# A graph layer's start on one core: the first loads put in one queue, and block 0's edges multiplied ahead of the weights' transposes

## The chip, the core and the metric

The kernel runs on one core of a Trainium2 chip. The core has five engines with queues of their own: PE (TensorE, matrix products; its weight loads are listed as PEld), DVE (VectorE), ACT (ScalarE), POOL (GpSimd) and SP (SyncE, which here only issues DMAs). [...] The metric is device time in microseconds (us) of one execution, as a median over runs.

## The reference, cut to what matters

There are 8192 nodes with 256 features and 131072 edges, sorted by their destination.

```python
ea  = edge_attr @ w_e + b_e                      # 131072 x 64 by 64 x 256
msg = relu(x[src] + ea)                          # a row of x for each edge
agg = segment_sum(msg, dst, num_segments=8192)
t = x + agg
h_local = bn1(relu(t @ w1 + b1) @ w2 + b2 + x)
q, k, v = split(x.reshape(256, 32, 256) @ in_w.T + in_b)   # 4 heads
h_attn = bn2(softmax(q k / 8) v @ out_w.T + out_b + x)
out = h_local + h_attn
out = bn3(out + relu(out @ m_w1 + m_b1) @ m_w2 + m_b2)
return layernorm(x + out)
```

Attention runs within groups of 32 nodes. All data is float32.

## The kernel before, in words

**Edges.** They are worked on in 128 blocks (NB) of 1024 edges. For each block:

- `gather` (L133) fetches the rows of x for the block's sources into a tile `xs`, in eight indirect DMAs that GpSimd issues, each of 128 rows of 1 KiB. Blocks 0 and 1 take their row numbers from `srcd`, loaded in small pieces at the very start (L64); all others from `srci`, which is made from `srci_r`: a cast to float (`srcf`, L193), eight PE transposes (L197), four casts back (L198). From block NX = 20 on they read `xb`, a copy of x with b_e added, so that the product with b_e is left out. There are four `xs` buffers: block b + 4 is gathered into the one that block b's messages were made from.
- `load_edges` (L148) brings the block's 64 edge attributes in four DMAs of 128 KiB into `ea` (two buffers), and `edge_transpose` (L166) turns them on DVE into `eaT` (two buffers).
- `edge_products` (L451) multiplies `eaT` with `we` on PE (L459, eight matmuls for a block; the trace shows each float32 matmul as two) and, up to block 19, adds `be` by a product with `sel` (L467).
- `edge_messages` (L478) adds `xs` on DVE (L487, two instructions) and takes the relu on ACT (L491).
- `edge_hot`, `edge_sums` and `edge_place` sum the messages by destination on PE (L510, L528) and add them to the transposed node features `xT` (L538).

`next_edges(b)` (L472) turns block b's attributes and loads those of block b + 2.

**Nodes.** They are worked on in 16 chunks of 512. `attention_front` (L274) loads `xn` (L276), turns it into `xT` on PE (L283, copies on ACT L284, L285) and makes q and k (L294); `attention_back` makes v (L308), scores (L325), the softmax and the output (L360, L372); `dense` is the rest (L391). These generators are drawn on by the class `Work` between the edge blocks.

**The copy xb.** `copy_load` (L550) loads pieces of x into `xp`, `copy_store` (L555) adds `be` on DVE (L558) and stores them.

**The order.** On PE the program's order is kept as written, and up to block NV = 26 on DVE and ACT too, once the main loop has begun; before it, and on SP, a scheduler orders by its own estimates. Every DMA of SP and ACT takes the next of eight semaphores and waits until the DMA that had it before has landed; the gathers do the same with eight of their own.

**The start.** SP issues half of srcd, the attributes of blocks 0 and 1, srci_r, dsti_r, the twelve vectors `vec_r` (L187), the attributes of blocks 2 and 3, then xn of chunks 0 and 1. ACT issues the other half of srcd, then we, be, in_r and out_r (L179 to L188). PE turns srcf, the projection weights (`turned`, L203: in_r, then out_r), the vectors and dstf, then xn of chunks 0 and 1, and only then comes block 0's `edge_products`. `turned` copies with ACT (L208). The destinations go through a cast (`dstf`, L232), two reductions (L237, L238) and a subtraction of the least (`lo`, L239) on DVE.

The main loop (L665) takes two blocks at a time up to TAIL = 104; after it a planner with due times (L697 on) orders single blocks.

Of the kernel before, what the change touches and what calls it, by code (L numbers as in the profile page):

```python
# [9 lines left out]
FP = mybir.dt.float32  # L10
# [14 lines left out]
NH = 4  # L25
# [28 lines left out]
def gnn_kernel(ctx: ExitStack, tc: tile.TileContext, x, src, dst, edge_attr, w, out):  # L54
# [102 lines left out]
                )  # L157

    gather(0)
    load_edges(0)  # L160
    gather(1)
    load_edges(1)

    eaT_of = {}

    def edge_transpose(b):  # L166
        ea = ea_of.pop(b)
        eaT = eaT_of[b] = epool.tile([P, NH * EQ, QR], FP, name="eaT", tag="eaT", bufs=2)
        nc.vector.transpose(eaT, ea[:, QR:].rearrange("p (g d) -> p g d", d=ED)[:, :, :QR])  # L169

    with tc.tile_pool(name="setup", bufs=1) as sp:


        srci_r = npool.tile([P, BE], I32, name="srci_r", tag="y")
        dsti_r = npool.tile([P, BE], I32, name="dsti_r", tag="h1")
        nc.sync.dma_start(srci_r, src.rearrange("(s e) -> s e", s=NB))
        nc.sync.dma_start(dsti_r, dst.rearrange("(s e) -> s e", s=NB))
        for h in range(2):
            nc.scalar.dma_start(we[h * ED : (h + 1) * ED, :], w["w_e"])  # L179
        nc.scalar.dma_start(be, w["b_e"][None, :].to_broadcast([P, C]))  # L180
        in_r = npool.tile([P, 3 * KC, C], FP, name="in_r", tag="m1")
        out_r = npool.tile([P, KC, C], FP, name="out_r", tag="vn")
        nc.scalar.dma_start(in_r, w["in_w"].rearrange("(o p) c -> p o c", p=P))
        vec_r = npool.tile([nrows, P], FP, name="vec_r", tag="pr")
        for v in VECS:
            r, n = col[v]
            nc.sync.dma_start(vec_r[r : r + n, :], w[v].rearrange("(r p) -> r p", p=P))  # L187
        nc.scalar.dma_start(out_r, w["out_w"].rearrange("(o p) c -> p o c", p=P))  # L188
        for b in range(2):
            edge_transpose(b)  # L190
            load_edges(b + 2)
        srcf = npool.tile([P, NH * TJ, EQ, QR], FP, name="srcf", tag="zT")
        nc.vector.tensor_copy(srcf, srci_r.rearrange("s (t r m) -> s t m r", r=QR, m=EQ))  # L193
        for h in range(NH):
            ps = bank()[:, : TJ * NB].rearrange("p (j s) -> p j s", j=TJ)
            for j in range(TJ):
                nc.tensor.transpose(ps[:, j, :], srcf[:, h * TJ + j].rearrange("s m r -> s (m r)"), ident)  # L197
            nc.vector.tensor_copy(srci[:, :, h * TJ : (h + 1) * TJ].rearrange("p s j -> p j s"), ps)  # L198


        nc.vector.memset(bd, 0.0)
# [70 lines left out]


    def attention_front(n0, st, pool, bank):  # L274
        xn = st["xn"] = pool.tile([P, TN, C], FP, name="xn", tag="xn", bufs=4)
        nc.sync.dma_start(xn, x[ds(n0, CH), :].rearrange("(t p) c -> p t c", p=P))  # L276
        yield REST
        xT = st["xT"] = pool.tile([P, KC, CH], FP, name="xT", tag="xT", bufs=4)
        hA = st["hA"] = pool.tile([P, KC, CH], FP, name="hA", tag="hA", bufs=4)
        for k in range(KC):  # L280
            ps = bank()
            for t in range(TN):
                nc.tensor.transpose(ps[:, t * P : (t + 1) * P], xn[:, t, k * P : (k + 1) * P], ident)  # L283
            nc.scalar.copy(xT[:, k, :], ps)  # L284
            nc.scalar.activation(  # L285
                hA[:, k, :], xT[:, k, :], AF.Identity, scale=s12[:, k : k + 1], bias=cA[:, k : k + 1]
            )
        yield 0.9

        qk = st["qk"] = pool.tile([P, 2 * KC, CH], FP, name="qk", tag="qk")  # L290
        for o in range(2 * KC):
            ps = bank()
            for k in range(KC):
                nc.tensor.matmul(  # L294
                    ps, inT[:, k, o * P : (o + 1) * P], xT[:, k, :], start=(k == 0), stop=(k == KC - 1)
                )
            nc.scalar.activation(qk[:, o, :], ps, AF.Identity, bias=v_("in_b", o))  # L297
            st["front"] = o == 2 * KC - 1
            yield 1.7
# [145 lines left out]
        yield 0.0  # L445


    chunk = [{} for _ in range(NCH)]
    pe_of, msg_of, oh_of, newest = {}, {}, {}, {}

    def edge_products(b):  # L451

        eaT = eaT_of.pop(b).rearrange("p (h m) r -> p h (m r)", h=NH)
        for h in range(0, NH, 2):
            pe = bank2().rearrange("p i (u c) -> p i u c", u=2)
            for u in range(2):
                for i in range(2):
                    rows = slice(i * ED, (i + 1) * ED)
                    nc.tensor.matmul(  # L459
                        pe[:, i, u, :], eaT[rows, h + u], we[rows, :],  # L460
                        start=(b >= NX or u == 0), stop=(b >= NX), skip_group_check=True,
                    )
            if b < NX:
                for u in range(2):
                    for i in range(2):
                        rows = slice(i * ED, (i + 1) * ED)
                        nc.tensor.matmul(  # L467
                            pe[:, i, u, :], sel[rows, :], be[rows, :], start=False, stop=True, skip_group_check=True
                        )
            pe_of[b, h] = pe  # L470

    def next_edges(b):  # L472
        if b < NB:
            edge_transpose(b)
        if b + 2 < NB:
            load_edges(b + 2)

    def edge_messages(b):  # L478

        xs = xs_of.pop(b)  # L480
        msg = msg_of[b] = epool.tile([P, NH, TJ, C], FP, name="msg", tag="msg", bufs=3)
        n = 2 if b < NB - 1 else 1
        for h in range(0, NH, 2):
            pe = pe_of.pop((b, h))
            for u in range(0, 2, n):
                hs = slice(h + u, h + u + n)
                nc.vector.tensor_add(  # L487
                    msg[:, hs].rearrange("p u i c -> p i u c"), pe[:, :, u : u + n, :],
                    xs[:, hs].rearrange("p u i c -> p i u c"),
                )  # L490
                nc.scalar.activation(msg[:, hs], msg[:, hs], AF.Relu)  # L491

    def edge_hot(b):

        oh = oh_of[b] = epool.tile([P, TB, WN], FP, name="oh", tag="oh", bufs=2)
        nc.vector.tensor_tensor(  # L496
            oh,
            iota_n[:, None, :WN].to_broadcast([P, TB, WN]),
            rel[:, b, :, None].to_broadcast([P, TB, WN]),
            ALU.is_equal,  # L500
        )

    def edge_sums(blocks):

        pw = pps.tile([P, 2, C], FP, name="pw", tag="pw", bufs=1)
        for i, b in enumerate(blocks):
            msg, oh = msg_of.pop(b), oh_of.pop(b)
            for j in range(TJ):
                for h in range(NH):
                    nc.tensor.matmul(  # L510
                        pw[h * WN : (h + 1) * WN, i, :], oh[:, h * TJ + j, :], msg[:, h, j, :],
                        start=(j == 0), stop=(j == TJ - 1), skip_group_check=True,
                    )
        n = len(blocks)
        ws = epool.tile([P, 2, C], FP, name="ws", tag="ws", bufs=2)
        newest["ws"] = nc.scalar.copy(ws[:, :n], pw[:, :n]).ins  # L516
        oh2 = epool.tile([P, 2, WB], FP, name="oh2", tag="oh2")
        for i, b in enumerate(blocks):
            nc.vector.tensor_scalar(oh2[:, i, :], iota_n, wrow[:, b : b + 1], None, ALU.is_equal)
        return blocks, ws, oh2  # L520

    def edge_place(blocks, ws, oh2):

        l2 = pps.tile([P, KC, C], FP, name="l2", tag="pw", bufs=1)
        last = len(blocks) - 1
        for i in range(last + 1):
            for k in range(KC):
                nc.tensor.matmul(  # L528
                    l2[:, k, i * NPB : i * NPB + WB], ws[:, i, k * P : (k + 1) * P], oh2[:, i, :],
                    start=(i == 0 and k == 0), stop=(i == last), skip_group_check=True,  # L530
                )
        n = blocks[0] * NPB - WL
        end = n + last * NPB + WB
        for c in range(max(n, 0) // CH, (min(end, N) - 1) // CH + 1):
            assert chunk[c]["v"]
            a, z = max(n, c * CH), min(end, (c + 1) * CH)
            xT = chunk[c]["xT"][:, :, a - c * CH : z - c * CH]
            newest["xT"] = nc.vector.tensor_add(xT, l2[:, :, a - n : z - n], xT).ins  # L538

    xp_of = {}  # L540


# [83 lines left out]
    with tc.manual_schedule(engines={PE}):  # L626
# [9 lines left out]
        for c in range(NCH):  # L636
            st, before, same = chunk[c], chunk[c - 1], chunk[c - 4]
            front = attention_front(c * CH, st, npool, bank)
            if c < 2:
                next(front)  # L640
                next(front)
            work.add(
                FRONT,
                lambda c=c, b=before, s=same: (c < 1 or b.get("scores"))
# [20 lines left out]
        while b < TAIL:  # L665
# [7 lines left out]
                    wt, name = ((w1, "w1"), (w2, "w2"), (mw1, "m_w1"), (mw2, "m_w2"))[i - 4]  # L673
                    nc.sync.dma_start(wt, w[name].rearrange("(k p) m -> p k m", p=P))

            edge_products(b)
            next_edges(b + 2)
            edge_messages(b)
            if waiting:
                sums = edge_sums(waiting)  # L680
            waiting = list(blocks)
# [185 lines left out]
```

## Time and profile before

| | |
|---|---|
| median of 3 runs | 1331.11 us (1328.47 to 1333.7) |
| the profiled execution | 1331.09 us |
| its span, first to last instruction | 1329.3 us |
| PE busy | 1195.2 us, 90% of the span |
| DVE busy | 784.9 us, 59% |
| ACT busy | 587.7 us, 44% |
| GpSimd (POOL) busy | 983.9 us, 74% |
| first 40 us: PE, DVE, POOL busy | 10.01, 16.43, 28.08 us |
| first 40 us: what the DMA engines moved | 224 GB/s |
| granted clock of PE, mean | 0.967 of full speed |

A row of the timeline gives the start, the duration, the engine (with a q for its queue of DMA issues), the source line, the operation, what is written from what, how many instructions were put together, and, in brackets, how long the engine was idle before and what ended that. A row of a group of instructions gives busy time and mean duration, then the idle time before them. What ended an idle time is inferred from semaphores, and where several were waited for it can name the wrong one.

### The profile page before, as it was taken

The page shows a single profiled execution, that of the slowest core. Times are in us where ns is not written, and L with a number is a line of the kernel's source. Part 1 is how long each engine was busy: PE and PEld are TensorE (multiplying, and loading weights), DVE is VectorE, ACT ScalarE, POOL GpSimd, SP SyncE. Part 2 cuts the span into 40 slices and gives each one's busy share as a digit, 9 for nine tenths or more (in the row PEclk, how much of TensorE's full clock was granted, in tenths as well). Part 3 has the DMA queues.
Part 4 walks back from the last instruction along what each step waited for, and adds up shares of the span by engine and source line. Part 5 has one row for each costly group of instructions (what it writes and reads, how often), then busy time and mean ns, then how long its engine had stood idle before and what let it go on. Part 6 is the DMA issues. An engine that isn't in the chain of part 4 may idle for free.

```text
span 1329.3 us, 21099 instructions
## 1 busy us (share of the span) xinstructions
PE 1195.2 (90%) x7795; PEld 741.0 (56%) x7795; DVE 784.9 (59%) x1339; ACT 587.7 (44%) x840; POOL 983.9 (74%) x1032
## 2 busy tenths in 40 slices
PE   2898989999998989899898988989898999999987
PEld 1566656556555556555555555545555555545655
DVE  4377555765756565755647465465646557575654
ACT  1343433454536454443435444354454444443433
POOL 6677777777777777777777777777777777777771
PEclk9899999999999989999999999989899999999998
DMA  7999966676667666666756666566566466656741
GB/s 204 320 267 299 260 199 169 169 199 167 181 160 196 157 181 167 171 177 165 190 150 185 160 176 171 157 181 167 170 169 199 138 169 186 166 163 159 192 129 47
DMA packets 148904, 240.34 MB, mean 181 GB/s; under 512 B 27934, under 2 KB 112188, under 8 KB 148028
## 3 DMA queue, kind: packets, MB, share of 16 engines
q0 software_dynamic: 49152, 134.28, 37.6%
q1 hardware_dynamic: 97196, 103.34, 28.9%
q10 hardware_dynamic: 2448, 1.32, 0.4%
q8 instruction: 63, 1.03, 0.3%
q14 instruction: 45, 0.37, 0.1%
HBM read 222.06 MB, written 16.78 MB: 180 GB/s over the span
## 4 chain that ended last, share of the span: by engine, by line
PE 38%; POOL 28%; issue 14%; DVE 9%; DMA 8%; ACT 2%; DVEq 0%; ACTq 0%; SPq 0%; POOLq 0%
POOL xs L138 28%; PE at L391 11%; PE pe L459 8%; DMA xs<-xb,srci 5%; PE at L294 5%; PE pw L510 4%; DVE msg L487 3%; PE l L528 3%; PE at L372 2%; PE pe L467 2%; PE at L308 1%; DMA xp<-in_x_dram 1%; PE at L360 1%; PE pe L325 1%; DMA in_r<-in_L_gnn_in_w_dram 1%
## 5 line engine op out<-in xcount | busy, mean ns | idle before, releaser
L138 POOL DMA_INDIRECT xs<-xb,srci x864 | 823.7, 953 | 263.2 <-issue 250.1
L491 ACT ACTIVATE msg<-msg 128x1024 f32<-128x1024 f32 (+1 forms) x258 | 270.0, 1049 | 435.5 <-DVE msg L487 432.6
L487 DVE TENSOR_TENSOR msg<-pe,xs 128x1024 f32<-128x1024 f32 (+1 forms) x258 | 305.7, 1199 | 155.4 <-DMA xs<-xb,srci 88.6
L459 PE MATMUL pe<-we,eaT 64*128 64x256 f32 x2048 | 271.0, 398 | 29.8 <-DVE msg L487 26.4
L459 PEld LDWEIGHTS pe<-we,eaT 64*128 64x128 f32 x2048 | 192.1, 191 | 118.5 <-issue 74.6
L138 POOL DMA_INDIRECT xs<-in_x_dram,srci x144 | 143.0, 993 | 48.8 <-issue 39.6
L169 DVE STREAM_TRANSPOSE eaT<-ea 128x512 f32<-128x512 f32 x128 | 90.1, 704 | 99.6 <-PE pe L459 70.9
L510 PE MATMUL pw<-msg,oh 128*32 128x256 f32 x2048 | 130.4, 389 | 6.6 <-DVE oh L496 5.0
L391 PE MATMUL at<-hA,mw 128*128 128x512 f32 (+2 forms) x304 | 123.9, 538 | 2.9 <-DVE hA L401 2.2
L294 PE MATMUL at<-xT,inT 128*128 128x512 f32 x256 | 120.9, 598 | 0.4 <-ACT xT L284 0.4
L391 PE MATMUL at<-m,mw 128*128 128x512 f32 (+2 forms) x304 | 117.5, 529 | 2.5 <-ACT qk L297 2.2
L510 PEld LDWEIGHTS pw<-msg,oh 128*32 128x32 f32 x2048 | 60.4, 111 | 69.1 <-issue 30.7
L528 PEld LDWEIGHTS l<-oh,ws 128*128 128x128 f32 x512 | 78.0, 196 | 28.4 <-issue 21.9
L528 PE MATMUL l<-oh,ws 128*128 128x160 f32 x512 | 87.9, 312 | 2.0 <-ACT ws L516 2.0
L391 PEld LDWEIGHTS at<-hA,mw 128*128 128x128 f32 x304 | 54.7, 196 | 50.5 <-issue 42.6
L391 PEld LDWEIGHTS at<-m,mw 128*128 128x128 f32 x304 | 54.2, 190 | 49.9 <-issue 44.5
L538 DVE TENSOR_TENSOR xT<-l,xT 128x96 f32<-128x96 f32 (+4 forms) x107 | 46.1, 452 | 54.2 <-PE l L528 53.9
L294 PEld LDWEIGHTS at<-xT,inT 128*128 128x128 f32 x256 | 47.0, 190 | 55.3 <-issue 51.0
L391 PE MATMUL at<-xT,w 128*128 128x512 f32 (+2 forms) x152 | 70.9, 606 | 6.9 <-DVE xT L538 6.9
L407 ACT ACTIVATE m<-at,vec 128x512 f32<-128x512 f32 (+2 forms) x76 | 46.8, 616 | 57.2 <-PE at L391 56.7
L297 ACT ACTIVATE qk<-at,vec 128x512 f32<-128x512 f32 x64 | 43.6, 684 | 62.6 <-PE at L294 62.4
L391 PE MATMUL at<-h,w 128*128 128x512 f32 (+2 forms) x152 | 64.2, 544 | 6.1 <-ACT h L398 6.1
(107 smaller groups left out, 1199.9 us busy)
## 6 DMA issues: line engine op xcount, KB each, us to landing
ea<-in_edge_attr_dram SPq DMA_DIRECT2D x512, 128.0 KB
xs<-xb,srci POOLq DMA_INDIRECT x864
xn<-in_x_dram SPq DMA_DIRECT2D x16, 512.0 KB
out_dram<-y SPq DMA_DIRECT2D x14, 512.0 KB
xp<-in_x_dram SPq DMA_DIRECT2D x10, 512.0 KB
xb<-xp SPq DMA_DIRECT2D x10, 512.0 KB
xp<-in_x_dram SPq DMA_DIRECT2D x3, 1024.0 KB
xb<-xp SPq DMA_DIRECT2D x3, 1024.0 KB
```

What stands on the lines that cost most here:

```text
L138: nc.gpsimd.indirect_dma_start(out=xs[:, h, j, :], out_offset=None, in_=x if b < NX else xb[:, :], in_offset=bass.IndirectOffsetOnAxis(ap= ...
L169: nc.vector.transpose(eaT, ea[:, QR:].rearrange("p (g d) -> p g d", d=ED)[:, :, :QR])
L294: nc.tensor.matmul(ps, inT[:, k, o * P : (o + 1) * P], xT[:, k, :], start=(k == 0), stop=(k == KC - 1))
L297: nc.scalar.activation(qk[:, o, :], ps, AF.Identity, bias=v_("in_b", o))
L391: nc.tensor.matmul(ps, wt[:, k, o * P : (o + 1) * P], act[:, k, :], start=(k == 0), stop=(k == nk - 1))
L407: nc.scalar.activation(m1[:, o, :], layer(mw1, KC, o, hA), AF.Relu, bias=v_("m_b1", o))
L459: nc.tensor.matmul(pe[:, i, u, :], eaT[rows, h + u], we[rows, :], start=(b >= NX or u == 0), stop=(b >= NX), skip_group_check=True,)
L487: nc.vector.tensor_add(msg[:, hs].rearrange("p u i c -> p i u c"), pe[:, :, u : u + n, :], xs[:, hs].rearrange("p u i c -> p i u c"),)
L491: nc.scalar.activation(msg[:, hs], msg[:, hs], AF.Relu)
L510: nc.tensor.matmul(pw[h * WN : (h + 1) * WN, i, :], oh[:, h * TJ + j, :], msg[:, h, j, :], start=(j == 0), stop=(j == TJ - 1), skip_group_ ...
L528: nc.tensor.matmul(l2[:, k, i * NPB : i * NPB + WB], ws[:, i, k * P : (k + 1) * P], oh2[:, i, :], start=(i == 0 and k == 0), stop=(i == la ...
L538: newest["xT"] = nc.vector.tensor_add(xT, l2[:, :, a - n : z - n], xT).ins
```

## The change: what it does

The loads of the start all go through SP, in the order srci_r, block 0's attributes, we, block 1's attributes, be, dsti_r, the vectors, in_r, xn of chunk 0, out_r, xn of chunk 1. Loading xn becomes a function of its own, called here for chunks 0 and 1. The attributes of blocks 0 and 1 are turned after srci is made, and block 0's products, the turn of block 2's attributes (with the load of block 4's) and block 0's messages are written ahead of the turning of the weights. The main loop leaves these three calls out for block 0. `edge_products` to `edge_place` stand earlier in the file, unchanged.

```diff
     gather(0)
-    load_edges(0)
     gather(1)
-    load_edges(1)
...
+    def load_nodes(n0, st, pool):
+        xn = st["xn"] = pool.tile([P, TN, C], FP, name="xn", tag="xn", bufs=4)
+        nc.sync.dma_start(xn, x[ds(n0, CH), :].rearrange("(t p) c -> p t c", p=P))
+
     with tc.tile_pool(name="setup", bufs=1) as sp:
         srci_r = npool.tile([P, BE], I32, name="srci_r", tag="y")
+        nc.sync.dma_start(srci_r, src.rearrange("(s e) -> s e", s=NB))
+        load_edges(0)
         dsti_r = npool.tile([P, BE], I32, name="dsti_r", tag="h1")
-        nc.sync.dma_start(srci_r, src.rearrange("(s e) -> s e", s=NB))
+        for h in range(2):
+            nc.sync.dma_start(we[h * ED : (h + 1) * ED, :], w["w_e"])
+        load_edges(1)
+        nc.sync.dma_start(be, w["b_e"][None, :].to_broadcast([P, C]))
         nc.sync.dma_start(dsti_r, dst.rearrange("(s e) -> s e", s=NB))
-        for h in range(2):
-            nc.scalar.dma_start(we[h * ED : (h + 1) * ED, :], w["w_e"])
-        nc.scalar.dma_start(be, w["b_e"][None, :].to_broadcast([P, C]))
         in_r = npool.tile([P, 3 * KC, C], FP, name="in_r", tag="m1")
         out_r = npool.tile([P, KC, C], FP, name="out_r", tag="vn")
-        nc.scalar.dma_start(in_r, w["in_w"].rearrange("(o p) c -> p o c", p=P))
...
             nc.sync.dma_start(vec_r[r : r + n, :], w[v].rearrange("(r p) -> r p", p=P))
-        nc.scalar.dma_start(out_r, w["out_w"].rearrange("(o p) c -> p o c", p=P))
-        for b in range(2):
-            edge_transpose(b)
-            load_edges(b + 2)
+        nc.sync.dma_start(in_r, w["in_w"].rearrange("(o p) c -> p o c", p=P))
+        load_nodes(0, chunk[0], npool)
+        nc.sync.dma_start(out_r, w["out_w"].rearrange("(o p) c -> p o c", p=P))
+        load_nodes(CH, chunk[1], npool)
...
+        for b in range(2):
+            edge_transpose(b)
+            load_edges(b + 2)
+        edge_products(0)
+        next_edges(2)
+        edge_messages(0)
...
     def attention_front(n0, st, pool, bank):
-        xn = st["xn"] = pool.tile([P, TN, C], FP, name="xn", tag="xn", bufs=4)
-        nc.sync.dma_start(xn, x[ds(n0, CH), :].rearrange("(t p) c -> p t c", p=P))
-        yield REST
+        if "xn" not in st:
+            load_nodes(n0, st, pool)
+            yield REST
+        xn = st["xn"]
...
             if c < 2:
                 next(front)
-                next(front)
...
-            edge_products(b)
-            next_edges(b + 2)
-            edge_messages(b)
+            if b:
+                edge_products(b)
+                next_edges(b + 2)
+                edge_messages(b)
```

In the built program SP's order is then: srcd, srci_r, attributes of block 0, we, attributes of block 1, be, dsti_r, the vectors, in_r, xn, out_r, xn, the attributes of blocks 2 to 5, and then the first two pieces of xp, which stood right behind xn before. DVE makes srci first, then turns the attributes of blocks 0 and 1, casts and reduces the destinations, makes block 0's messages, and goes on with the destinations. From block 1's messages on, the order on PE, DVE and ACT is as before.

More of the change, by code (lines that the diff above doesn't have):

```diff
@@ L169, in edge_transpose, with edge_products @@
         nc.vector.transpose(eaT, ea[:, QR:].rearrange("p (g d) -> p g d", d=ED)[:, :, :QR])
+    pe_of, msg_of, oh_of, newest = {}, {}, {}, {}
+    def edge_products(b):
+        eaT = eaT_of.pop(b).rearrange("p (h m) r -> p h (m r)", h=NH)
+        for h in range(0, NH, 2):
+            pe = bank2().rearrange("p i (u c) -> p i u c", u=2)
+            for u in range(2):
+                for i in range(2):
+                    rows = slice(i * ED, (i + 1) * ED)
+                    nc.tensor.matmul(
+                        pe[:, i, u, :], eaT[rows, h + u], we[rows, :],
+                        start=(b >= NX or u == 0), stop=(b >= NX), skip_group_check=True,
+                    )
+            if b < NX:
+                for u in range(2):
+                    for i in range(2):
+                        rows = slice(i * ED, (i + 1) * ED)
+                        nc.tensor.matmul(
+                            pe[:, i, u, :], sel[rows, :], be[rows, :], start=False, stop=True, skip_group_check=True
+                        )
+            pe_of[b, h] = pe
@@ new lines, in next_edges, with edge_messages @@
+    def next_edges(b):
+        if b < NB:
+            edge_transpose(b)
+        if b + 2 < NB:
+            load_edges(b + 2)
+    def edge_messages(b):
+        xs = xs_of.pop(b)
+        msg = msg_of[b] = epool.tile([P, NH, TJ, C], FP, name="msg", tag="msg", bufs=3)
+        n = 2 if b < NB - 1 else 1
+        for h in range(0, NH, 2):
+            pe = pe_of.pop((b, h))
+            for u in range(0, 2, n):
+                hs = slice(h + u, h + u + n)
+                nc.vector.tensor_add(
+                    msg[:, hs].rearrange("p u i c -> p i u c"), pe[:, :, u : u + n, :],
+                    xs[:, hs].rearrange("p u i c -> p i u c"),
+                )
+                nc.scalar.activation(msg[:, hs], msg[:, hs], AF.Relu)
@@ new lines, in edge_hot, with edge_sums @@
+    def edge_hot(b):
+        oh = oh_of[b] = epool.tile([P, TB, WN], FP, name="oh", tag="oh", bufs=2)
+        nc.vector.tensor_tensor(
+            oh,
+            iota_n[:, None, :WN].to_broadcast([P, TB, WN]),
+            rel[:, b, :, None].to_broadcast([P, TB, WN]),
+            ALU.is_equal,
+        )
+    def edge_sums(blocks):
+        pw = pps.tile([P, 2, C], FP, name="pw", tag="pw", bufs=1)
+        for i, b in enumerate(blocks):
+            msg, oh = msg_of.pop(b), oh_of.pop(b)
+            for j in range(TJ):
+                for h in range(NH):
+                    nc.tensor.matmul(
+                        pw[h * WN : (h + 1) * WN, i, :], oh[:, h * TJ + j, :], msg[:, h, j, :],
+                        start=(j == 0), stop=(j == TJ - 1), skip_group_check=True,
+                    )
+        n = len(blocks)
+        ws = epool.tile([P, 2, C], FP, name="ws", tag="ws", bufs=2)
+        newest["ws"] = nc.scalar.copy(ws[:, :n], pw[:, :n]).ins
+        oh2 = epool.tile([P, 2, WB], FP, name="oh2", tag="oh2")
+        for i, b in enumerate(blocks):
+            nc.vector.tensor_scalar(oh2[:, i, :], iota_n, wrow[:, b : b + 1], None, ALU.is_equal)
+        return blocks, ws, oh2
@@ new lines, in edge_place @@
+    def edge_place(blocks, ws, oh2):
+        l2 = pps.tile([P, KC, C], FP, name="l2", tag="pw", bufs=1)
+        last = len(blocks) - 1
+        for i in range(last + 1):
+            for k in range(KC):
+                nc.tensor.matmul(
+                    l2[:, k, i * NPB : i * NPB + WB], ws[:, i, k * P : (k + 1) * P], oh2[:, i, :],
+                    start=(i == 0 and k == 0), stop=(i == last), skip_group_check=True,
+                )
+        n = blocks[0] * NPB - WL
+        end = n + last * NPB + WB
+        for c in range(max(n, 0) // CH, (min(end, N) - 1) // CH + 1):
+            assert chunk[c]["v"]
+            a, z = max(n, c * CH), min(end, (c + 1) * CH)
+            xT = chunk[c]["xT"][:, :, a - c * CH : z - c * CH]
+            newest["xT"] = nc.vector.tensor_add(xT, l2[:, :, a - n : z - n], xT).ins
@@ L171, in gnn_kernel @@
+    chunk = [{} for _ in range(NCH)]
+    def load_nodes(n0, st, pool):
+        xn = st["xn"] = pool.tile([P, TN, C], FP, name="xn", tag="xn", bufs=4)
+        nc.sync.dma_start(xn, x[ds(n0, CH), :].rearrange("(t p) c -> p t c", p=P))
     with tc.tile_pool(name="setup", bufs=1) as sp:
         srci_r = npool.tile([P, BE], I32, name="srci_r", tag="y")
+        nc.sync.dma_start(srci_r, src.rearrange("(s e) -> s e", s=NB))
+        load_edges(0)
         dsti_r = npool.tile([P, BE], I32, name="dsti_r", tag="h1")
-        nc.sync.dma_start(srci_r, src.rearrange("(s e) -> s e", s=NB))
+        for h in range(2):
+            nc.sync.dma_start(we[h * ED : (h + 1) * ED, :], w["w_e"])
+        load_edges(1)
+        nc.sync.dma_start(be, w["b_e"][None, :].to_broadcast([P, C]))
@@ L198, in gnn_kernel @@
             nc.vector.tensor_copy(srci[:, :, h * TJ : (h + 1) * TJ].rearrange("p s j -> p j s"), ps)
+        for b in range(2):
+            edge_transpose(b)
+            load_edges(b + 2)
+        edge_products(0)
+        next_edges(2)
+        edge_messages(0)
         nc.vector.memset(bd, 0.0)
@@ L445, in dense @@
         yield 0.0
[L448 to L538, printed above, removed]
```

## The prediction

> **What bounds the kernel.** I read the page first, then GpSimd's timeline, its waits, and the timeline of the first 60 us.
>
> ```profile
> span 1329.3 us, 21099 instructions
> ...
> PE 1195.2 (90%) x7795; PEld 741.0 (56%) x7795; DVE 784.9 (59%) x1339; ACT 587.7 (44%) x840; POOL 983.9 (74%) x1032
> ...
> L138 POOL DMA_INDIRECT xs<-xb,srci x864 | 823.7, 953 | 263.2 <-issue 250.1
> ```
>
> By busy share the tensor engine leads (90%), GpSimd has 74%. But a gather is 0.95 us of busy time and 0.30 us of "issue" that belongs to it (250.1 of 263.2 us idle): a pace of 1.25 us, and there are 1024. The gathers' own timeline tells whether that pace is ever broken (columns: start, duration, engine, what, and the idle time before):
>
> ```profile
> 4.25 1.10 POOL L138 DMA_INDIRECT xs<-in_x_dram,srcd  x1 [2.65 <-issue]
> ...
> 23.16 1.80 POOL L138 DMA_INDIRECT xs<-in_x_dram,srcd  x1 [0.30 <-issue]
> 25.87 1.47 POOL L138 DMA_INDIRECT xs<-in_x_dram,srci  x1 [0.92 <-DVE srci L198]
> 27.65 0.95 POOL L138 DMA_INDIRECT xs<-in_x_dram,srci  x1 [0.30 <-issue]
> ...
> 45.14 0.94 POOL L138 DMA_INDIRECT xs<-in_x_dram,srci  x1 [0.30 <-issue]
> 49.30 0.94 POOL L138 DMA_INDIRECT xs<-in_x_dram,srci  x1 [3.22 <-DVE msg L487]
> ...
> 73.19 2.29 POOL L138 DMA_INDIRECT xs<-in_x_dram,srci  x1 [0.30 <-issue]
> ```
>
> ```profile
> 194.43 0.94 POOL L138 DMA_INDIRECT xs<-in_x_dram,srci  x1 [0.30 <-issue]
> ...
> 197.06 0.96 POOL L138 DMA_INDIRECT xs<-in_x_dram,srci  x1 [1.68 <-DVE oh L519]
> ```
>
> The last gather starts at 1302.79. From 4.25, 1023 steps of 1.25 us come to 1283.0; 19.8 us are lost on the way. The steps shown give 1.46 us (to 25.87), 0.53 (to 27.65), 2.91 (to 49.30) and 1.38 (to 197.06), together 6.3. The rest is some forty gathers longer than 0.95 us, such as that at 73.19. After 197.06 no wait over 0.31 us is listed. From the last gather to the end are 26.5 us. So **GpSimd's queue of gathers sets the end**: what it loses, the kernel loses, as long as the buffers (xs, four of them) come free in time. That the chain of waits gives PE 38% says that PE is close behind, not that it is the bound.
>
> Why does it wait? At 25.87 for indices (srci). At 49.30 and 197.06 for an xs buffer: block 4 needs the one that block 0's two adds (L487) read, block 18 that of block 14.
>
> ```profile
> 15.26 0.43 SPq L176 DMA_DIRECT2D srci_r<-in_src_dram  x1
> ...
> 26.95 3.65 SPq L154 DMA_DIRECT2D ea<-in_edge_attr_dram  x8
> ...
> 30.64 0.98 SPq L276 DMA_DIRECT2D xn<-in_x_dram  x2
> ...
> 37.80 1.94 PE L283 MATMUL at<-ident,xn 128*128 128x128 f32 x8 [2.75 <-DMA xn<-in_x_dram]
> ...
> 46.08 0.71 DVE L169 STREAM_TRANSPOSE eaT<-ea 128x512 f32<-128x512 f32 x1 [10.11 <-DMA xp<-in_x_dram]
> 46.72 2.32 DVE L487 TENSOR_TENSOR msg<-pe,xs 128x1024 f32<-128x1024 f32 x2
> ...
> 51.70 7.13 PE L294 MATMUL at<-xT,inT 128*128 128x512 f32 x16
> ```
>
> Block 0's gathers were issued by 14.1, yet its adds ran at 46.72: PE's products of block 0 (42.26) stand behind the transposes of xn (37.80), and xn was asked for at 30.64, because SP spent 12.54 us on eight ea issues and then stood in the small vec loads until 26.95. In the later stretch the adds trail too: block 14's end at 196.8 although its gathers were issued by 164.1. Between 40 and 200 us the list of PE's waits names only 0.7 us for a DMA, so there **PE's order of work, started late, holds the buffers**.
>
> **The change part by part**, against the profiled execution (1331.09 us, of which the span is 1329.3; the median of the runs is 1331.11, so the same sum serves both).
>
> 1. srci_r becomes SP's first load after srcd: issued at about 2.7 instead of 15.26. In before it was cast at 23.06, 7.8 us after its issue; the same 7.8 make it about 10.5, the four srci copies end near 14, and gather 16 is not due until some 25. The wait of 0.92 falls to the usual 0.30: **0.6 us gained**. What is late next is nothing near: 11 us of room.
>
> 2. The casts stay beside gathers. [...] The row agrees for the casts: the gather beside the cast srcf (23.06, 1.07 us) took 1.80 instead of 0.95, the one beside dstf (25.45) 1.47. So srcf costs its 0.85 again elsewhere; dstf, half of which now fell into the wait, goes from 0.53 to 0.85: **0.3 lost**. [...]
>
> 3. Block 0's 8+8 products, its two adds and relus move ahead of the weights' transposes. They need ea0, we, be and block 0's gathers. The gathers decide: issued by 14.1, and landed within 10 us, since each gather waits for the eighth before it and no such wait shows. So the adds run at 20 to 25, and gather 32, due near 45, finds its buffer 20 us free: **2.9 us gained**. Behind these adds DVE holds the dst subtraction and the vec copy, behind the relus ACT holds the copies of in_w's transposes; both have room until the weights land.
>
> 4. Five loads go from ACT's queue to SP's. ACT saves 2.7 us of issue (0.45 to 0.60 each) before 5.65, where it next works at 27.82: worth nothing. SP pays them, but the 29 issues from srci_r to xn1, at 0.45 us or less each, are 13 us, under the transfers. Both kernels need the same 5.4 MiB (srci_r, dsti_r, ea0 to ea3, we, be, in_r, out_r, xn0, xn1) at the start; before had them all with xn1 at 40.39 (PE's second xn transposes), an average of about 150 GB/s from 2.7 us. At that rate xn1, now with 1 MiB less ahead of it, lands at about 33, and ea3, now last, at about 40.
>
> 5. So PE's order starts earlier. After: xn1's transposes end near 35.5, block 1's products (3.8 us) near 39.5, and the first L294 starts there instead of 51.70: **a lead of up to 12 us**. Block 1's adds now stand behind the eaT transposes of blocks 2 and 3, so behind ea3: 40 + 0.7 + 2.3 gives about 43.5; gather 40 needs them at 55.9. Nothing that PE consumes is missing for this lead: block 9's adds ran at 129.66, its last gather was issued at 109.9 and landed before 120.
>
> 6. The third stall: gather 144 (block 18) now arrives 3.2 us earlier, at 192.2, and needs block 14's adds done 4.6 us earlier than before; block 16's first (174.7) needs block 12's 2.9 us earlier. With a lead of 12, shrinking to perhaps 6 under way, both hold: **1.4 us gained**. From there on the order on PE, DVE and ACT is the same instruction for instruction, and in many blocks past 570 us, and in the last four, the adds end within 3 to 6 us of the block's last gather, so PE has caught up by then: all of it moves with the gathers, the last 26.5 us too.
>
> 7. SP's order further on: ea4 and ea5 now stand ahead of the xp loads, which go from 32.26 to about 42, after the transposes of block 3. With 1 MiB of ea ahead of the first pair's 1.5 they land between 55 (at 195 GB/s: the 300 GB/s of the stretch from 40 to 80 us less 105 for the gathers, 128 KiB per 1.25 us) and 60 (at 150). Their add ran at 72.39 and would now like to run at 60: it may cost DVE a microsecond of the lead, of which 7 are spare. xn2 and xn3 move from 55.69 to about 80 to 95, used at 129.77; w1 moves to about 65, used at 203.00. All hidden; without that cover each microsecond would eat the lead before it costs time.
>
> Sum: -0.6 + 0.3 - 2.9 - 1.4 = **-4.6 us**, 1331.1 - 4.6 = **1326.5**. The ends: -6 (dstf beside no gather, the adds on xp beside fewer) and 0 (no lead at all).
>
> **The rivals.** (a) The stall only moves: if PE's lead at block 12 is below 4.6 us, gathers 128 and 144 wait for xs as before, and the gain is the lead itself; at 2.5 us the time is 1328.6. For it: PE is 34 to 38 us busy of every 40 from 40 to 200, so a lead lost is not made up. Against it: the 12 us of step 5. (b) Fewer long gathers: between 70 and 185 seven gathers beside other work of DVE (73.19 and its like) cost 5.9 us over 0.95. With DVE's adds on xp at other phases half of that may go: 1326.5 - 3 = 1323.5. But the same adds still run beside gathers without a pause, so it can as well go the other way. (c) **Slower: the xp loads come late.** In DVE's fixed order the add on xp stands ahead of block 4's messages. From that add's start to the end of block 4's adds are 14.1 us in before (72.39 to 86.5), and gather 64, which waits for them, started at 90.8. A landing at 78 ends them at 92: 1.3 us late against before, which the third stall (1.4) just pays back, so this is where it decides; a landing at 86 ends them at 100, 9.4 late, and the time is 1331 + 8 = 1339. For it: they are pushed behind two more blocks of edges in a single queue, with the DMA engines' share at 1.07 and 1.02 in the stretches 40 to 80 and 80 to 120. Against it: that is 18 us over the later of the two estimates. (d) The change does not do what it says: excluded by the built order, which has block 0's products before in_r's transposes.
>
> **The numbers.** About 0.5% (6.7 us) can be told from no change here. Forecast 0.64, (a) 0.16, (b) 0.13, (c) 0.07. The range takes in (b) with 1 us of scatter below, 1322.5, and most of (a) above, to 1330.8, just short of no gain; the runs of before alone lie 5.3 us apart. Faster by over 0.5% (below 1324.4): (b) and a little of the forecast's edge, 0.19; slower (c) mostly, 0.06; the rest, 0.75, is within.
>
> **What would show it.** Gathers' timeline: no idle over 0.31 us near 25, 46 and 195, the last gather near 1298.2, and still 26.5 us behind it. DVE's first two adds at 20 to 25; PE's first L294 near 39.5; srcf cast near 10. A wait for DVE msg at gathers 40 to 150 would be (a), and a DVE idle before L558's new line, with a DMA of xp as its end, would be (c). I am wrong if the last gather starts within a microsecond of 1302.8, or if the tail behind it changes.

## The result, and the profile after

The changed kernel takes 1327.49 us (median of 22 runs, 1324.36 to 1329.69), the kernel before in the same measurement 1330.32 us (22 runs): a ratio of 0.9972, 95% interval 0.9963 to 0.998. That is 2.8 us less, where 4.6 were forecast. The profiled run took 1327.67 us.

The page of the changed kernel, its span and the row of the gathers:

```profile
span 1325.9 us, 21105 instructions
...
L138 POOL DMA_INDIRECT xs<-xb,srci x864 | 824.1, 954 | 263.2 <-issue 246.5
```

Its idle time, 263.2 us, is what it was before, to the tenth: the row holds only the 864 gathers from xb (blocks 20 to 127), and what has moved lies ahead of them and shows only in the timeline. The new line numbers: L208 is the message add, L167 the transposition eaT, L180 and L188 the products, L401 the old L294, L432 the old L325, L345 the subtraction of lo.

GpSimd's timeline of the changed kernel, at the places that the prediction named (start, duration, idle before):

```profile
8.12 1.43 POOL L138 DMA_INDIRECT xs<-in_x_dram,srcd  x1 [0.30 <-issue]
...
17.37 1.67 POOL L138 DMA_INDIRECT xs<-in_x_dram,srcd  x1 [0.30 <-issue]
...
23.09 1.71 POOL L138 DMA_INDIRECT xs<-in_x_dram,srcd  x1 [0.30 <-issue]
...
26.36 0.95 POOL L138 DMA_INDIRECT xs<-in_x_dram,srci  x1 [0.30 <-issue]
...
46.36 0.94 POOL L138 DMA_INDIRECT xs<-in_x_dram,srci  x1 [0.30 <-issue]
```

```profile
190.74 0.95 POOL L138 DMA_INDIRECT xs<-in_x_dram,srci  x1 [0.30 <-issue]
194.64 0.97 POOL L138 DMA_INDIRECT xs<-in_x_dram,srci  x1 [2.96 <-DVE oh L240]
```

The stall at gather 32 is gone (46.36, idle 0.30) and so is the wait for srci at gather 16 (26.36). But three gathers of the start are long, and gather 144 waits 2.96 us where before it waited 1.68. Everything that the gathers lose over 1.25 us a step, by place:

| place | before | after | change | forecast |
|---|---|---|---|---|
| gathers 1 to 31 | 2.14 | 2.14 | 0.0 | -0.3 |
| gather 32 | 2.91 | 0.00 | -2.91 | -2.9 |
| gathers 33 to 143 | 6.38 | 5.63 | -0.75 | 0 |
| gather 144 | 1.38 | 2.65 | +1.27 | -1.4 |
| gathers 145 to 1023 | 6.98 | 7.35 | +0.37 | 0 |
| behind the last gather | 26.5 | 25.2 | -1.35 | 0 |

(The table is the sum of each gather's start less the one before and less 1.25. With 0.03 at the first gather it comes to -3.4, the difference of the two spans.) The largest miss: gather 144 was to gain 1.4 us and lost 1.3.

Why? The head start was there. The timeline of all engines:

```profile
7.66 1.07 DVE L291 CAST srcf<-srci_r 128x1024 f32<-128x1024 int32 x1 [4.12 <-DMA srci_r<-in_src_dram]
...
20.51 2.34 DVE L208 TENSOR_TENSOR msg<-pe,xs 128x1024 f32<-128x1024 f32 x2
...
36.40 5.42 PE L401 MATMUL at<-xT,inT 128*128 128x512 f32 x12
```

PE's first L401 runs 15.3 us earlier than L294 did (51.70), and message block 6 still 13.5 us earlier (89.5 against 103.0). Block 7 is 9.4 us earlier (99.2 against 108.5), block 10 only 2.9 (145.4, 148.3), block 14, whose buffer gather 144 needs, 2.4. Its two adds, before and after:

```profile
194.47 2.32 DVE L487 TENSOR_TENSOR msg<-pe,xs 128x1024 f32<-128x1024 f32 x2
```

```profile
192.06 2.32 DVE L208 TENSOR_TENSOR msg<-pe,xs 128x1024 f32<-128x1024 f32 x2
```

Gather 144 would have come 5.1 us earlier than its buffer came free before, so it waits 2.65 of them. The lead is lost between 93 and 145 us. VectorE, then TensorE, in that stretch:

```profile
98.53 0.71 DVE L167 STREAM_TRANSPOSE eaT<-ea 128x512 f32<-128x512 f32 x1 [6.07 <-DMA ea<-in_edge_attr_dram]
...
117.44 0.71 DVE L167 STREAM_TRANSPOSE eaT<-ea 128x512 f32<-128x512 f32 x1 [2.63 <-DMA ea<-in_edge_attr_dram]
```

```profile
95.16 1.99 PE L415 MATMUL at<-inT,xT 128*128 128x256 f32 x8
100.50 3.79 PE L432 MATMUL pe<-qk 64*128 64x128 f32 x32 [3.35 <-DVE msg L208]
...
114.62 3.64 PE L231 MATMUL pw<-msg,oh 128*32 128x256 f32 x32 [4.25 <-DVE oh L217]
```

VectorE stood idle 6.07 us before the transposition at 98.53, for the edge attributes of block 9, and another 2.63 before that at 117.44, for those of block 10; before, the list of VectorE's waits had no DMA of ea between 40 and 240 us. TensorE, behind it, paused 3.35 us, and then L432 took 3.79 us where L325 had taken 2.06. The windows of 2 us say why (columns: PE, PEld, DVE, ACT, POOL busy, the granted clock, DMA share, GB/s):

```profile
98.00:100.00 2.00, 0.00 (x0) 0.00 (x0) 1.47 (x2) 0.00 (x0) 1.59 (x2) 0.96 0.92 327
100.00:102.00 2.00, 1.50 (x14) 1.53 (x16) 2.00 (x3) 1.54 (x2) 1.50 (x2) 0.50 0.73 228
102.00:104.00 2.00, 2.00 (x22) 1.99 (x20) 2.00 (x2) 1.92 (x5) 1.70 (x2) 0.50 1.09 325
104.00:106.00 2.00, 2.00 (x11) 1.78 (x8) 1.41 (x2) 1.55 (x5) 1.70 (x2) 0.50 0.80 284
106.00:108.00 2.00, 2.00 (x15) 1.56 (x16) 1.22 (x2) 0.00 (x0) 1.39 (x3) 0.83 1.07 312
```

TensorE comes out of the pause at half its clock (0.50) and stays there until about 106.7. The clock fell within the pause of 3.35 us: if it went from 1.00 to 0.50 in one step, the 0.96 of the first window puts that about 0.2 us before 100, some 2.7 us after the pause began.

And why did the edges come late? SP's queue in the changed kernel:

```profile
64.00 1.73 SPq L688 DMA_DIRECT2D w<-in_L_gnn_w_dram  x2
...
72.92 2.54 SPq L154 DMA_DIRECT2D ea<-in_edge_attr_dram  x4
75.65 1.58 SPq L688 DMA_DIRECT2D mw<-in_L_gnn_m_w_dram  x2
81.06 5.37 SPq L154 DMA_DIRECT2D ea<-in_edge_attr_dram  x4
```

The four matrices of the dense layers (w, mw: 1.5 MiB, first used at 200.5 us) are issued around the edges of block 8 (72.92), and ahead of those of block 9 (81.06 to 86.4). Before, they went out at 35 to 55 us. The diff does not touch them: the scheduler moved them. The DMA engines' mean share is 0.95 to 1.07 in each 40 us from 40 to 160 us, in both kernels.

Of the seven occasions on which the experiments ran, five had the kernel before itself at 1995 to 2034 us instead of 1329, for a reason that was not found, and the times of those ten runs (e1 to e6, e8 to e11) decide nothing here.

So two causes stood in line: **A**, the loads of the weights make the edges late and these eat the lead; **B**, the clock falls for reasons of its own. A third, **C**, is a form of A: every byte in the full stretch costs its time, wherever it stands in the queue.

### The profile page after: what moved, and what is told of

It is laid out like the page before. It is cut to its first block, busy times and chain, and to the rows that moved or that the text cites. A ratio compares the mean times of both kernels' runs of the same rounds, so it can differ in the third digit from the quotient of the medians.

```text
span 1325.9 us, 21105 instructions
## 1 busy us (share of the span) xinstructions
PE 1201.6 (91%) x7795; PEld 744.8 (56%) x7795; DVE 785.4 (59%) x1339; ACT 587.3 (44%) x840; POOL 984.2 (74%) x1032
## 3 DMA queue, kind: packets, MB, share of 16 engines
q8 instruction: 63, 1.03, 0.3%
## 4 chain that ended last, share of the span: by engine, by line
PE 39%; POOL 23%; issue 12%; DMA 12%; DVE 9%; ACT 3%; SPq 1%; DVEq 0%; POOLq 0%; ACTq 0%
POOL xs L138 23%; PE at L498 12%; PE pe L180 8%; DMA xs<-xb,srci 5%; PE at L401 5%; PE pw L231 4%; DVE msg L208 4%; PE l L249 3%; PE at L479 2%; DMA ea<-in_edge_attr_dram 2%; DMA xs<-in_x_dram,srci 2%; PE at L415 1%; PE at L467 1%; PE pe L188 1%; DMA xb<-xp 1%
## 5 line engine op out<-in xcount | busy, mean ns | idle before, releaser
L138 POOL DMA_INDIRECT xs<-xb,srci x864 | 824.1, 954 | 263.2 <-issue 246.5
L208 DVE TENSOR_TENSOR msg<-pe,xs 128x1024 f32<-128x1024 f32 (+1 forms) x258 | 305.4, 1199 | 152.3 <-DMA xs<-xb,srci 86.3
L180 PE MATMUL pe<-we,eaT 64*128 64x256 f32 x2048 | 273.5, 401 | 30.6 <-DVE msg L208 26.0
L180 PEld LDWEIGHTS pe<-we,eaT 64*128 64x128 f32 x2048 | 193.9, 192 | 120.2 <-issue 74.9
L167 DVE STREAM_TRANSPOSE eaT<-ea 128x512 f32<-128x512 f32 x128 | 90.2, 704 | 88.1 <-PE pe L180 68.0
L231 PE MATMUL pw<-msg,oh 128*32 128x256 f32 x2048 | 130.2, 388 | 5.8 <-DVE oh L217 4.3
L401 PE MATMUL at<-xT,inT 128*128 128x512 f32 x256 | 122.8, 605 | 2.0 <-ACT qk L404 1.5
L231 PEld LDWEIGHTS pw<-msg,oh 128*32 128x32 f32 x2048 | 60.0, 111 | 68.4 <-issue 29.8
L401 PEld LDWEIGHTS at<-xT,inT 128*128 128x128 f32 x256 | 47.3, 191 | 57.7 <-issue 51.2
L432 PE MATMUL pe<-qk 64*128 64x128 f32 x512 | 42.9, 321 | 31.5 <-DVE msg L208 31.5
```

What stands on the lines that cost most here:

```text
L138: nc.gpsimd.indirect_dma_start(out=xs[:, h, j, :], out_offset=None, in_=x if b < NX else xb[:, :], in_offset=bass.IndirectOffsetOnAxis(ap= ...
L180: nc.tensor.matmul(pe[:, i, u, :], eaT[rows, h + u], we[rows, :], start=(b >= NX or u == 0), stop=(b >= NX), skip_group_check=True,)
L208: nc.vector.tensor_add(msg[:, hs].rearrange("p u i c -> p i u c"), pe[:, :, u : u + n, :], xs[:, hs].rearrange("p u i c -> p i u c"),)
L231: nc.tensor.matmul(pw[h * WN : (h + 1) * WN, i, :], oh[:, h * TJ + j, :], msg[:, h, j, :], start=(j == 0), stop=(j == TJ - 1), skip_group_ ...
L401: nc.tensor.matmul(ps, inT[:, k, o * P : (o + 1) * P], xT[:, k, :], start=(k == 0), stop=(k == KC - 1))
```

## The experiments

The times of e7 and e12 count. From the other ten runs only rows are used: the lengths of single gathers, which are the same there (0.95 us), and in e9 the order. The changed kernel was not run beside e7 or e12; each is compared with before.

### The weights' loads late

```diff
-                if 4 <= i < 8:
+                if 14 <= i < 18:
...
-                    nc.sync.dma_start(wt, ...)
+                    with tc.issue_after(last_ea[b + 3]):
+                        nc.sync.dma_start(wt, ...)
```

(The loads of xn are tied to the edges of block 9 in the same way, so that they keep their place.) e2 and e5 are the same kernel, with times that decide nothing (0.9982, interval 0.9944 to 1.002; 0.9987, 0.9947 to 1.0026).

> The changed kernel with the four weights' loads put behind the edge loads of blocks 17 and 19 in SP's queue (issued at about 170 and 190 us, first use at 200.5), everything else in the same order. Theory A: as with the weights left out up to 165 us, stall at gather 144 gone, 1324.8 us (0.995); a first dense layer that waits for w1 shows on TensorE at 200 and costs the gathers nothing. Theory B: 1327.5 (0.997), clock row as in the changed kernel.

> The same kernel as e5 (the four weights' loads behind the edge loads of blocks 17 and 19 in SP's queue, at about 170 and 190 us), on another occasion, since the kernel before took some 2000 us both times. Theory A (the loads, ahead of ea 8 and ea 9 in the full DMA stage, eat the lead of the messages over the gathers): VectorE's wait of 6.07 us for ea before the transpose at 98.53 goes, message block 14 starts at 184 to 186 instead of 192.1, the stall of 2.66 us at gather 144 goes, 1324.8 us, 0.9952 of before. Theory B (TensorE's granted clock, 0.67 to 0.83 from 100 to 140 us, falls for reasons of its own and eats the lead): the ea wait goes, clock row and stall stay, 0.9972.

Measured, e7: 1323.99 us against 1328.91, a ratio of 0.9962, interval 0.9951 to 0.9973. GpSimd, and SP, in e7:

```profile
191.74 0.95 POOL L138 DMA_INDIRECT xs<-in_x_dram,srci  x1 [0.30 <-issue]
193.00 0.95 POOL L138 DMA_INDIRECT xs<-in_x_dram,srci  x1 [0.30 <-issue]
```

```profile
70.31 9.59 SPq L154 DMA_DIRECT2D ea<-in_edge_attr_dram  x8
...
170.79 2.11 SPq L690 DMA_DIRECT2D w<-in_L_gnn_w_dram  x2
...
191.04 1.29 SPq L690 DMA_DIRECT2D mw<-in_L_gnn_m_w_dram  x2
```

Gather 144 (193.00) does not wait. The edges of blocks 8 and 9 leave at 70.31 to 79.9, VectorE's waits for ea are gone from its list, TensorE does not pause at 97, message block 7 runs at 94.0 (99.2), block 8 at 108.7 (118.1), block 14 at 181.7 (192.1). That is what A expected, even 2 us better; and B falls as a cause of its own, since the half clock at 100 went with the pause. TensorE still pauses there once, 5.00 us, for oh before L231 at 108.01, as before did at 122.56, and is at half clock (0.50) until about 113.6. Of the expected 2.7 us on the changed kernel, medians show 2.1 (4.9 against 2.8 below before); the two intervals overlap, so that part rests on the trace, one execution of each. Its span is 4.2 us shorter. The gathers up to 144 explain 1.7 of them: 2.65 at gather 144 and 0.6 at the start are gained, 1.56 lost at gathers 33 to 143. Another 2.4 come from many small steps behind gather 144 (4.96 us lost there, in e12 5.16, in the changed kernel 7.35), which A did not foresee; why is open.

### The weights not loaded, or loaded first

In e1 ScalarE fills the four tiles from inT, so the dense layers compute with other numbers; in e3 the loads come with blocks 0 to 3 (both with the same tie of xn):

```diff
-                if 4 <= i < 8:
+                if 0 <= i < 4:
```

> The changed kernel without the four loads of w1, w2, mw1, mw2 (1.5 MiB at 64 to 77 us): ScalarE fills the four tiles with parts of inT instead, so the dense layers work on other numbers. All else stands in the same order on every engine and queue. Theory A (in the full DMA stage these loads, standing in SP's queue ahead of ea 8 and ea 9, make the edge blocks late, and the lead of the messages over the gathers is eaten): 1.5 MiB at the some 190 GB/s that the gathers leave of 300 are 8 us, so ea 9 is issued by 78 instead of 86, VectorE's wait for ea before the transpose at 98.53 (6.07 us) goes, message block 14 starts at 184 to 186 instead of 192.1, the stall of 2.66 us at gather 144 goes, and the time is 1324.8 us, 0.995 of before. Theory B (the granted clock of TensorE, 0.67 to 0.83 from 100 to 140 us, falls for reasons of its own): the ea waits go but the clock row stays, message block 14 still starts after 190, and the time is 1327.5, 0.997.

> The changed kernel with the four weights' loads four blocks earlier in SP's queue (about 38 to 46 us, around the first xp loads), the same bytes before 160 us. Theory A in its narrow form (the place in the queue counts: ahead of ea 8 and ea 9 it hurts, earlier the lead of 13 us covers it): lead kept, stall at gather 144 gone, 1324.8 us. Theory C (the DMA engines are full from 40 to 160 us, and every byte in that stretch costs its time wherever it stands): the xp loads and with them ea 8 and ea 9 are as late as now, message block 14 after 190, stall at gather 144 of 2 to 3 us, 1327.5; slower than the changed kernel by up to 2 us if ea 4 or ea 5 also come late enough for a second stall.

Measured: 1.0008 (0.9981 to 1.0035) and 0.9992 (0.9953 to 1.003): no verdict. What e3 was to tell, e12 told in part, with the same bytes early but a smaller lead at the start.

### The loads alone

Block 0's products and messages go back into the main loop; the single queue stays.

```diff
-        edge_products(0)
-        next_edges(2)
-        edge_messages(0)
...
-            if b:
-                edge_products(b)
-                next_edges(b + 2)
-                edge_messages(b)
+            edge_products(b)
+            next_edges(b + 2)
+            edge_messages(b)
```

Three runs of it (e8, e10, e11) have no verdict: 0.9993 (0.9962 to 1.0023), 0.9968 (0.9929 to 1.0006), 1.001 (0.9976 to 1.0044).

> The kernel of e10 once more: all first loads in SP's queue in order of need, block 0's products and messages back in the main loop, behind the weights' transposes. If the loads carry the gain: messages 0 run by about 40 (before 46.7), the stall of 2.91 us at gather 32 is gone, and the time is 0.9975 to 0.9985 of before. If the early messages carry it: messages 0 end after 45, gather 32 still waits 1 us or more, 0.999 or above. Stall at gather 144, with the weights' loads around the first xp loads (ahead of ea 6, the same bytes before 160 us): below 1.4 us if the place in the queue alone eats the lead, 2 us or more if every byte in the full DMA stage costs its time.

Measured, e12: 1324.42 us against 1329.34, 0.9967, interval 0.9955 to 0.9979: a little more than the 0.9975 to 0.9985 that was expected. VectorE's and GpSimd's timelines in e12:

```profile
36.02 2.32 DVE L208 TENSOR_TENSOR msg<-pe,xs 128x1024 f32<-128x1024 f32 x2
```

```profile
45.19 0.94 POOL L138 DMA_INDIRECT xs<-in_x_dram,srci  x1 [0.30 <-issue]
```

```profile
191.89 0.95 POOL L138 DMA_INDIRECT xs<-in_x_dram,srci  x1 [0.30 <-issue]
```

Messages 0 run at 36.02, 10.7 us earlier than before, and gather 32 (45.19) finds its buffer free: **the loads alone are enough for the whole gain**. With them, putting block 0's messages forward to 20.5 gains nothing more, since no one waits for them before 45. What the early messages would gain without the loads is not shown. And gather 144 (191.89) does not wait, though the lead at the start was smaller (first L398, the old L294, at 41.01 instead of 36.40). SP's queue, VectorE and TensorE:

```profile
48.08 2.35 SPq L685 DMA_DIRECT2D w<-in_L_gnn_w_dram  x2
50.79 0.37 SPq L685 DMA_DIRECT2D mw<-in_L_gnn_m_w_dram  x1
...
58.75 0.39 SPq L685 DMA_DIRECT2D mw<-in_L_gnn_m_w_dram  x1
...
80.57 10.54 SPq L154 DMA_DIRECT2D ea<-in_edge_attr_dram  x8
```

```profile
93.86 0.71 DVE L167 STREAM_TRANSPOSE eaT<-ea 128x512 f32<-128x512 f32 x1 [4.29 <-DMA ea<-in_edge_attr_dram]
```

```profile
95.83 1.13 PE L180 MATMUL pe<-we,eaT 64*128 64x256 f32 x8 [1.47 <-DVE msg L208]
...
101.41 2.06 PE L429 MATMUL pe<-qk 64*128 64x128 f32 x32
...
113.39 3.64 PE L231 MATMUL pw<-msg,oh 128*32 128x256 f32 x32 [4.98 <-DVE oh L217]
```

Here the scheduler issued the weights at 48 to 59, the same bytes ahead of the edges of block 8 (80.57), and these are late too: VectorE idles 4.29 us at 93.86, and message block 7 runs at 99.4, just when it does in the changed kernel (99.2). So far this fits C: with these bytes ahead, block 7 runs at some 99 in both kernels, though their leads at the start differ by 4.6 us; e7, without them, has it at 94.0. But what follows differs. TensorE pauses 1.47 us (95.83), stays at full clock (1.00), does the old L325 at 101.41 in 2.06 us, and has one long pause, the 4.98 us for oh that every kernel has here. From block 7 to block 14 it takes 87.6 us, e7 87.7, before 85.9, the changed kernel 92.9. Of the 5.3 us between the changed kernel and e12 here, 4.2 fall between blocks 7 and 8 (18.9 us against 14.8): 2.6 are VectorE's wait for the edges of block 10 (117.44), which come in time in e12, and the rest lies beside the half clock of 99.8 to 106.7. Another 1.7 fall between blocks 9 and 10, beside a further such stretch (130.6 to 134.0). So B has up to 3 us in it, though at 100 the clock fell in the pause that the late edges made. As a forecast of the time C fell: 2 us or more of stall expected, none found.

### The subtraction on ScalarE

```diff
-        nc.vector.tensor_sub(dst3, dst3, lo[...].to_broadcast(...))
+        nlo = sp.tile([P, NH], FP, name="nlo")
+        nc.vector.tensor_scalar(nlo, lo, -1.0, None, ALU.mult)
+        for h in range(NH):
+            nc.scalar.activation(dst3[:, h], dst3[:, h], AF.Identity, bias=nlo[:, h : h + 1])
```

> The changed kernel with the subtraction of lo from dst (one VectorE instruction with two SBUF inputs, 1.21 us at 22.77) done by ScalarE in four pieces with a bias. If the two SBUF inputs hold the gather beside it (1.71 us at 23.09): that gather falls to 0.95 us, the gap total of the first 30 us falls from 1.97 to 1.2 us, and, the gathers being the bound, the time falls by 0.8 us to 1326.7 (0.9966), less what the later stall at gather 144 takes back, since its slot does not come free any earlier: nothing then, 1327.5. If it was chance, the gather stays near 1.7 us.

> The changed kernel with the subtraction of lo from dst (one VectorE instruction with two SBUF inputs, 1.21 us at 22.77) done by ScalarE in four pieces with a bias, run again for the same reason. If the two SBUF inputs hold the gather beside it (1.71 us at 23.09): that gather falls to 0.95 us and the gap total of the first 30 us from 1.97 to 1.2 us; the time falls by 0.8 us to 0.9966 of before if nothing later takes it back, and stays at 0.9972 if the stall at gather 144 grows by as much, since its slot does not come free earlier. If it was chance, the gather stays near 1.7 us.

Measured: 0.9975 (0.9944 to 1.0005) and 0.9946 (0.9905 to 0.9987). In these runs the gathers were not the bound (in e4 GpSimd idled some 640 us before them beyond the usual 0.30 each), so that the times say nothing of 0.8 us. The gathers' lengths do. ScalarE and GpSimd in e4, then the same place with the subtraction on VectorE, in e1:

```profile
33.64 1.69 ACT L348 ACTIVATE dstf<-dstf,nlo 128x256 f32<-128x256 f32 x4
```

```profile
32.99 0.95 POOL L138 DMA_INDIRECT xs<-in_x_dram,srci  x1 [0.30 <-DVE over L358]
34.25 0.94 POOL L138 DMA_INDIRECT xs<-in_x_dram,srci  x1 [0.30 <-issue]
35.50 0.95 POOL L138 DMA_INDIRECT xs<-in_x_dram,srci  x1 [0.30 <-issue]
```

```profile
30.52 1.22 DVE L345 TENSOR_TENSOR dstf<-dstf,lo 128x1024 f32<-128x1024 f32 x1
30.63 1.93 POOL L138 DMA_INDIRECT xs<-in_x_dram,srci  x1 [0.30 <-issue]
```

Beside ScalarE's four pieces the gathers keep 0.95 us (in e6 too); beside VectorE's subtraction the held one took 1.93 in e1, 1.31 in e2, 1.71 in e3, 1.02 in e5, 1.84 in e9, 1.52 in e8, 1.53 in e10 and e11, 1.16 in e7, and 1.71 in the changed kernel; in before and e12 none was held. So the subtraction did hold a gather in these runs, for 1.02 to 1.93 us instead of 0.95; that its two SBUF inputs are the reason is not shown, and whether taking it away shortens the kernel was not settled.

### The messages alone

The kernel before, with its two queues, and block 0's products and messages put forward (the three calls behind the copies to srci, and "if b:" in the loop).

> The second half alone: the kernel before with its two queues and its order of loads, block 0's products and messages put ahead of the weights' transposes. On VectorE the first message add of block 0 now stands ahead of the cast of src: it waits for the first half of gather block 0 (landed at 16.0) and for be on ScalarE's queue, so the cast starts some 1.2 us later than before and gather 16, which waits for srci (0.53 us over its pace), waits 1 to 3 us longer. Messages 0 end by 25, the stall of 2.91 us at gather 32 is gone unless message block 1 or TensorE's later work moves it on. If the early messages carry the gain: minus 2.9 plus 1 to 3: 1328.5 to 1330.5 (0.9985 to 1.0). If the two halves need each other, it is slower than before: 1331 to 1333 (1.0005 to 1.002).

Measured: 0.9987 (0.9944 to 1.003), no verdict. Its first 40 us show the order that was expected (the first add at 27.15, the cast of src behind it at 28.30) and a wait longer by more than the 1 to 3 us expected (gather 16 idle 6.96 us before 31.11, in before 0.92). How long that wait is in a run of 1330 us, and so what this half does alone, stays open.

## Why the prediction was right, and why its size was off

The time lies in the range, and the largest term, the stall at gather 32, came as forecast. But the course was that of rival (a), given 0.16, and not that of the forecast, given 0.64: the lead at block 12 was 2.9 us, below the 4.6 named there, gather 144 waited, and it came earlier than before by just the lead at block 14, 2.4 us (197.06, 194.64). That the time came out between those two cases is partly luck: of the 3.4 us by which the span fell, 1.35 lie behind the last gather, where the prediction counted nothing and named any change as a sign that it is wrong. By its steps:

1. Right. The cast of src ran at 7.66 (about 10.5 expected), gather 16 idled 0.30.
2. **Mis-sized.** The casts cost 0.48 and 0.73 of their 0.85 each, but the subtraction of lo, for which the sum has no term, cost 0.76 (the gather at 23.09, 1.71 instead of 0.95), where the row of before, two gathers of 0.94 and 0.95, gave nothing. That row was a matter of phase (last section). With the 0.76 the sum is -3.8.
3. Right in time (the adds at 20.51), and worth nothing beside the loads: in e12 the same 2.9 us come with the adds at 36.02.
4. Right. The single queue held nothing up in the first 40 us; the xn transposes began at 30.81. (The loads named add up to 5.25 MiB, not 5.4, so the rate was 146 GB/s; nothing hangs on it.)
5. Right, and more: PE's L401 at 36.40 where 39.5 was expected.
6. **This step failed**: "With a lead of 12, shrinking to perhaps 6 under way, both hold". The lead began at 15.3 and shrank to 2.4 at block 14, below the 4.6 needed (5.1 as it turned out); the term was -1.4 and measured +1.3. This is rival (a), at gather 144 alone: gather 128, for which 2.9 us were said to be needed, got 2.9 and did not wait. e7 and e12 show the step's own logic sound: where the lead at block 14 is 12.8 or 7.6, the wait is gone.
7. **The cause of 6**: "w1 moves to about 65 ... All hidden". The weights did move to 64, and their first use was as far off as said. What was not asked is who stands behind them: in full DMA engines (a mean share of 1.06 and 1.03 in the stretches 40 to 80 and 80 to 120), the edges of blocks 8 and 9, and behind those VectorE, and TensorE, which after its pause of 3.35 us worked at 0.50 of its clock until about 106.7. "It may cost DVE a microsecond of the lead" was said of xp; from block 6 to block 14 the lead lost 11.

Rival (b) came in part (-0.75 before gather 144, +0.4 after). Rival (c) did not: VectorE's list has 2.1 us that end with a transfer of xp, before it had 10.1. The tail was to stay at 26.5 and is 25.2, in e7 and e12 25.0. The clock tells most of it. The same instruction in the tail, before and after:

```profile
1308.84 1.94 PE L510 MATMUL pw<-msg,oh 128*32 128x256 f32 x16
```

```profile
1307.55 1.07 PE L231 MATMUL pw<-msg,oh 128*32 128x256 f32 x16
```

From 1307 to 1314 the mean granted clock was 0.51 before; after, from 1306 to 1313, it was 1.00. The same 32 matmuls (from L391 at 1307.69 to the next L391 at 1314.34; after, 1306.87 to 1310.73) took 6.65 us before and 3.86 after; 1.2 us of that went again because they began that much later behind the last gather. Whether the change has a part in this, or before's profiled execution was unlucky there, is open.

## What to carry to other kernels

A lead is no sum to be carried forward: follow it through the first stretch in which the DMA engines are full, and list every load that the new order puts ahead of the one needed next, also those that the diff does not name. When two edits come together, ask which of them the nearest deadline needs: here one of the two, ordering the loads by need, was enough alone. A single row without contention is one draw of the phase: beside the same subtraction a gather took 0.94 us in before and 1.93 in e1. Price it between the two.

## What the runs showed of the hardware

**Gathers beside VectorE.** Fourteen profiles show the two casts and, but for two of them, the subtraction. In these a gather that started 0.1 to 1.02 us into any of the three ended 0.82 to 0.84 us after that instruction's end: in the changed kernel the subtraction ends at 23.98 and the gather at 24.80. A gather that started up to 0.50 us ahead of a cast ended 0.12 us after the cast (e7: cast to 8.22, gather from 6.92 to 8.33), and so did one that started 0.01 us behind it (e10); one that started ahead of the subtraction, by 0 to 0.93 us, was not touched (0.94 us in before, 0.95 in the changed kernel and e12). That made the row of before:

```profile
30.15 0.94 POOL L138 DMA_INDIRECT xs<-in_x_dram,srci  x1 [0.30 <-issue]
30.16 1.25 DVE L239 TENSOR_TENSOR dstf<-dstf,lo 128x1024 f32<-128x1024 f32 x1
...
31.40 0.95 POOL L138 DMA_INDIRECT xs<-in_x_dram,srci  x1 [0.30 <-issue]
```

The gather at 30.15 had begun 0.01 us ahead, the next one 0.01 us before the end. e12 repeats it (20.17 and 20.19). Beside a subtraction of 1.21 to 1.25 us, at a pace of 1.25 us, a gather lost nothing (before, e12) or up to 0.98 us (e1), by phase alone. So the subtraction held only gathers that started during it, the casts also some that had begun up to 0.50 us ahead of them, and a cast ahead of which the gather had begun still kept its 1.07 to 1.09 us.

**The clock.** In the traces of before, the changed kernel, e7 and e12, between 90 and 142 us, TensorE works at 0.50 after each pause of 3.35 to 5.0 us (before, e7 and e12 once, the changed kernel twice), for some 3.4 to 9.1 us, and not after the pause of 1.47 in e12. The clock falls 2.7 to 5.1 us after the pause has begun. The changed kernel has a third such stretch at 130.6 to 134.0, after pauses of only 1.7 and 0.2 us; before, e7 and e12 have the same two pauses there (1.71 and 0.22 us) at full clock (1.00). So in these traces the length of the pause does not by itself tell whether the clock falls.
